# Layer 0 of a four-layer graph kernel: VectorE's work for a row's own sum ranked ahead of its other work, small side products and rank sums issued one row later

## Chip, cores and metric

The kernel runs on one core of a Trainium2 chip. The metric is the device time of one execution in microseconds (us): the median of three runs. Before the change it is 1355.77 us (1353.71 to 1357.23).

## What is computed

`x` is 2708 x 512, `adj` is a sparse, symmetrically placed 2708 x 2708 matrix with a diagonal. Four layers follow each other; each takes `h = relu(layernorm(x))`, does a graph operation with it and adds the result to `x`. The change touches layer 0 alone:

```python
h = jnp.maximum(_layernorm(x), 0.0)
mask = adj > 0
head = mask / sqrt(sum(mask * mask, axis=-1))      # one number per row, on the entries
inc = adj + head
x = x + (inc @ h) / sum(inc, axis=-1)
```

Layer 1 is an attention with the mask of `adj`, which this kernel serves by taking, for each row, the value row of its largest entry. Layer 2 is two products with `adj`, layer 3 one product with `adj != 0` divided by column counts. Layers 1 to 3 also use the lists of nonzero columns that layer 0 makes.

## The kernel before

**Tiles and stages.** The 2708 rows make 22 tiles of 128 rows (the last has 20); I call a tile of rows a row. Layer 0 is one Python loop over `m` in 0 to 21 (L854 to L912), written out in full. Each pass emits the sum of row `m` on TensorE (L865 to L869): first the products with whole tiles of `adj_t` (`inc`), then those with gathered columns (`incl`). All 22 tiles are whole for rows 0 to 2 (`LEAD`); later rows take 6 down to 0 whole tiles (`WHOLE`) and 5 to 8 gathered chunks (`CHUNKS`; row 21 takes 2). For each piece VectorE makes `inc = (a > 0) * rb + a` in `add_head`, with two instructions: L698 and L706. `incidence(m + 1)` (L688), which holds these, is emitted ahead of the sum of row `m`.

**What follows a row's sum.** VectorE adds it to `x` (L879), then `norm` (L191) takes its statistics (L194, L196, L199, L201, with a square root and the final scaling on ScalarE, L198 and L204). The result `hn` is transposed on TensorE one pass later (`after`, L210) and multiplied with the value weights two passes later (L176). `yo` (L810) is then stored to the DRAM table `y`, which layer 1 gathers from.

**Statistics of later rows.** In the same pass `stats_to` (L762) does the statistics of a row that lies up to eight further on: sign and counts on ScalarE (`row_norm`, L583, L587), the row's sum on ScalarE (`row_sum`, L611), the row's largest entry and its place on VectorE (`attended`, L622 to L624). In `row_norm`, for rows 6 to 20, the 128 x 128 block on the diagonal is taken care of at once: VectorE clears the diagonal in the sign block (L592) and picks the diagonal (L595), TensorE multiplies the sign block with a column of ones (L599), and VectorE turns that into `diag_c` (L600).

**Lists of nonzero columns.** After every third row, `count` (L315) adds up the signs of the three rows on TensorE (L325) and ScalarE copies the counts (L341, L343, L345). `rank_blocks` (L391) follows at once: VectorE takes the block sums `rk`, `sums` (L399), TensorE adds the blocks ahead with `ahead_of` (L403), ScalarE copies that (L404), VectorE scans (L405) and sets the end (L406), and SP issues four stores to `rank_b` (L409). Later passes read the ranks back (`load_ranks`, L445) and find the columns (`search`, L448, with the instruction L461); `do_next` (L751) takes one job from the queue `todo` for each row of statistics. `gathers_to(m + 2)` (L790) then has GpSimd gather the entries of row `m + 3` (`gather_adj`, L635) and the rows of `h` of row `m + 2` (`gather_rows`, L654).

**End of layer 0.** From row 14 on, rows 3, 4, 5, 0, 1, 2 (`LATE`), whose slabs were given up, are loaded again and get their signs counted (`count_signs`, L565, held back by a one-element copy of the current `xt`, L182) and their largest entry found. The ranks of row 21 and of rows 1 and 2 are made in `rank_rows` with a long scan (L424); the columns of rows 1 and 2 are searched and gathered for the later layers, and a weight is split in three (L215 to L225). Then `idx` is copied (L914), and layer 1 begins with gathers of `y` by `idx` (L1172).

**What sets the order.** Each engine has one queue in a fixed order. That order is made when the program is built: a planner runs through it with its own estimates of durations, and takes for each engine, of the instructions that are ready by these estimates, the one with the lowest number `tc.cur_priority`. This number grows in the order in which the Python code emits. `tc.issue_after(ins)` adds that what the block emits on the engine of `ins` stands behind it in the queue.

Of the kernel before, what the change touches and what calls it, by code (L numbers as in the profile page):

```python
# [2 lines left out]

# [6 lines left out]
FP = mybir.dt.float32  # L10
# [7 lines left out]
ALU = mybir.AluOpType  # L18
# [17 lines left out]

DENSE = 6
LEAD = 3
HEAD = 3
WHOLE = (6, 6, 6, 6, 6, 6, 4, 4, 4, 4, 4, 4, 3, 3, 3, 4, 4, 4, 3, 3, 3, 0)  # L40
CHUNKS = (0, 10, 9, 8, 7, 7, 7, 7, 7, 6, 6, 6, 6, 6, 6, 5, 5, 5, 5, 5, 5, 2)
# [3 lines left out]
def kernel(  # L45
# [181 lines left out]
    def split_w(pool, raw, tag, first=None):  # L227
# [5 lines left out]
            split_b(*(part[:, c, :] for part in w), raw[:, c, :])  # L233
        return w

    short = ctx.enter_context(ExitStack())
    wset = short.enter_context(tc.tile_pool(name="wset", bufs=1))

# [5 lines left out]
    with tc.tile_pool(name="l0_slab", bufs=2) as slabs, tc.tile_pool(  # L244
# [146 lines left out]
        def rank_blocks(ms, last_block):  # L391

            wide = layout(ms[0] // GROUP)[1]
            row_end = hp.tile([P, WIDE + 1], HF, name="rk")
            rk, end = row_end[:, :wide], row_end[:, wide : wide + 1]
            sums, offs = (wp.tile([P, 1], FP, name=name) for name in ("sums", "offs"))
            nc.vector.tensor_scalar(  # L399
                rk, last_block, 1.0, None, op0=ALU.min, op1=ALU.add, accum_out=sums  # L400
            )
            ahead = ps_list.tile([P, BLK], FP, name="list")
            nc.tensor.matmul(ahead[:, :1], ahead_of, sums, start=True, stop=True)  # L403
# [168 lines left out]
        def row_norm(m):  # L572


            n = rows(m)
            ar = slab[m]

            cnt, sum_sgn = cnts[:, m : m + 1], sums_sgn[:, m : m + 1]
            if m in LATE:
                cnt = sum_sgn = wp.tile([P, 1], FP, name="sum_sgn", bufs=4)  # L580
            rn, deg = (wp.tile([P, 1], FP, name=name, bufs=10) for name in ("rn", "deg"))
            sgn = slabs.tile([P, N], BF, name="sgn", bufs=GROUP)
            nc.scalar.activation(sgn[:n], ar[:n], AF.Sign, accum_out=sum_sgn[:n])  # L583
            if m in LATE:
                nc.vector.tensor_scalar_max(cnt[:n], cnt[:n], 0.0)
            else:
                nc.scalar.activation(sgn[:n], sgn[:n], AF.Relu, accum_out=cnt[:n])  # L587
            nc.scalar.activation(rn[:n], cnt[:n], AF.Sqrt, bias=tiny[:n])
            nc.vector.reciprocal(rn[:n], rn[:n])
            if alone(m):  # L590
                cols = slice(m * P, (m + 1) * P)
                nc.vector.tensor_tensor(sgn[:, cols], sgn[:, cols], off_diag, ALU.mult)  # L592
                picked = wp.tile([P, P], FP, name="dg")
                d = diag[:, m : m + 1]
                nc.vector.scalar_tensor_tensor(  # L595
                    picked, ar[:, cols], 1.0, ident, op0=ALU.mult, op1=ALU.mult, accum_out=d
                )
# [90 lines left out]
        def incidence(m):  # L688

            n = rows(m)  # L690
            rn = row[m][0]
            rb = ps_small.tile([P, P], FP, name="rb")
            nc.tensor.matmul(
                rb[:, :n], rn[:n].to_broadcast([n, P]), ident[:n, :n], start=True, stop=True
            )

            def add_head(inc, a, k, num):
                nc.vector.scalar_tensor_tensor(  # L698
                    inc,
                    a,  # L700
                    0.0,
                    rb[:k, :n].unsqueeze(1).to_broadcast([k, num, n]),
                    op0=ALU.is_gt,
                    op1=ALU.mult,
                )
                nc.vector.tensor_tensor(inc, inc, a, ALU.add)  # L706

            pairs = []
            if m >= LEAD:
                ts = tiles_d[: dense_of(m)]  # L710
                pieces = [ts[i : i + PIECE0] for i in range(0, len(ts), PIECE0)]
            else:
                pieces = in_order if m + 1 < LEAD else dense_last
            for ts in pieces:
                at, k = blocks.pop(m) if m in blocks else load_block(m, ts)
                d = (slice(0, k), slice(0, len(ts)), slice(0, n))
                inc = slabs.tile([P, PIECE0, P], FP, name="inc", bufs=3)
                add_head(inc[d], at[d], k, len(ts))
                pairs += [(inc[:k, i, :n], h0[t][:k]) for i, t in enumerate(ts)]
            if alone(m):  # L720
                c = diag_c[:, m : m + 1]
                by = wp.tile([P, 3], FP, name="by")
                nc.scalar.activation(by[:, 2:3], c, AF.Sign)
                nc.scalar.activation(by[:, 2:3], by[:, 2:3], AF.Identity, scale=rn, bias=c)
                nc.scalar.activation(by[:, :2], kept[:, :, m], AF.Copy, scale=by[:, 2:3])
                own = wp.tile([P, D], FP, name="own", bufs=1)
                nc.scalar.activation(own, xs[m], AF.Relu, scale=by[:, 0:1], bias=by[:, 1:2])
                pairs.append((ident, own))
            if m >= LEAD:
                ac, gs = gathers.pop(m)  # L730
# [15 lines left out]
        listable = set()  # L746


        todo = []
# [12 lines left out]
        def stats_to(m):  # L762


            while normed[0] <= order_n.index(m):
# [88 lines left out]
        for m in range(NT):  # L854
# [10 lines left out]
            for i, (a, g) in enumerate(pairs):  # L865
                product = nc.tensor.matmul(  # L866
                    acc[:n], a, g, start=(i == 0), stop=(i == len(pairs) - 1)
                )
                first_of_sum = first_of_sum if i else product.ins  # L869
            if m + 1 < LEAD:  # L870
                stats_to(m + 1)
                incs[m + 1] = incidence(m + 1)
            if m > 1:
                with tc.issue_after(first_of_sum):
# [4 lines left out]
            nc.vector.scalar_tensor_tensor(  # L879
                xt[:n], acc[:n], row.pop(m)[1][:n], xt[:n], op0=ALU.mult, op1=ALU.add  # L880
            )
# [1071 lines left out]
```

## Time and profile before

| | us |
|---|---|
| median of three runs | 1355.77 |
| the profiled execution, whole | 1431.05 |
| its span, first to last instruction | 1429.2 |
| TensorE busy in the span | 1218.8 (85%) |
| VectorE busy | 924.7 (65%) |
| ScalarE busy | 693.2 (49%) |
| GpSimd busy | 673.6 (47%) |
| mean granted TensorE clock | 0.925 |

The last sum of layer 0 ends at 488 us of the span, and the first product of layer 1 starts at 526.91 us.

How to read it: a group's row gives line, engine, operation, what is written and read, count, busy time, mean duration, then the idle time of that engine just before, and what ended it. "PE" is TensorE, "PEld" its weight loads, DVE VectorE, ACT ScalarE, POOL GpSimd, SP the engine that only issues transfers. A float32 product shows as two MATMUL records. In the list of waits a row reads: who waited, for whom, us in total, times, the longest. In a timeline: start, busy time, engine, line, operation, and in brackets the idle time before and what ended it. In the table by stretches: bounds, length, then busy time of PE, PEld, DVE, ACT, POOL, the granted TensorE clock, the busy share of the transfer engines and GB/s. "remote" as a releaser means that the trace knows a semaphore's update but no work or transfer that made it at that time.

### The profile page before, as it was taken

To read this page: it belongs to the slowest core of one execution; us is meant where nothing else is said; L and a number is where in the kernel's file an instruction comes from. 1 tells how busy PE (TensorE), PEld (TensorE's weight loads), DVE (VectorE), ACT (ScalarE), POOL (GpSimd) and SP (SyncE) were. 2 spreads that over 40 slices of the span, in tenths; PEclk is the share of its full clock that TensorE was granted. 3 is DMA by queue.
4 is the path that set the end of the run, shared out by engine and by line. 5 is a ranking of instruction groups with operands and counts; after the bars stand their busy time and mean duration, and the time that the engine had idled before them with its cause. 6 is when DMAs were issued, how large, how long until landed. Compare 5 with 4: busy or idle time off the path is not lost. (4 is left out here: it accounts for less than half of the span.)

```text
span 1429.2 us, 15148 instructions
## 1 busy us (share of the span) xinstructions
PE 1218.8 (85%) x4223; PEld 726.3 (51%) x4223; DVE 924.7 (65%) x1859; ACT 693.2 (49%) x1098; POOL 673.6 (47%) x703
## 2 busy tenths in 40 slices
PE   4985977769896848999989999899999999958797
PEld 2332433324343326765655655466666666646575
DVE  4664977768899857952343446356667685746576
ACT  5873563648635636642232224245555554634353
POOL 2245457555667441116645543245445344167663
PEclk9977998789988969999999999999999999979898
DMA  9976898778979477638888887856566666488785
GB/s 342 350 251 225 283 302 277 246 249 293 322 253 335 168 254 266 220 128 272 259 261 255 274 248 239 273 177 219 194 212 193 198 190 207 137 313 249 248 250 163
DMA packets 179342, 349.92 MB, mean 245 GB/s; under 512 B 22795, under 2 KB 85525, under 8 KB 175517
## 3 DMA queue, kind: packets, MB, share of 16 engines
q1 hardware_dynamic: 131648, 201.72, 41.5%
q0 software_dynamic: 46032, 145.05, 32.6%
q10 hardware_dynamic: 1568, 2.10, 0.4%
q8 instruction: 35, 0.57, 0.2%
q14 instruction: 59, 0.48, 0.1%
HBM read 285.97 MB, written 62.82 MB: 244 GB/s over the span
## 5 line engine op out<-in xcount | busy, mean ns | idle before, releaser
L1047 POOL DMA_INDIRECT gg<-g2d,idx_g x130 | 141.2, 1086 | 197.1 <-PE aggs L1110 149.3
L1110 PE MATMUL aggs<-gg,ac 128*128 128x512 f32 (+1 forms) x520 | 231.3, 593 | 3.2 <-DMA gg<-g1d,idx_g 2.1
L1047 POOL DMA_INDIRECT gg<-g1d,idx_g x130 | 130.7, 1005 | 159.1 <-PE aggs L1110 86.5
L635 POOL DMA_INDIRECT ac<-in_adj_t_dram,idx_a x130 | 132.7, 1021 | 91.9 <-issue 37.3
L866 PE MATMUL acc<-h,inc 128*128 128x512 f32 (+1 forms) x276 | 143.0, 664 | 37.4 <-DVE inc L706 29.2
L1110 PEld LDWEIGHTS aggs<-gg,ac 128*128 128x128 f32 (+1 forms) x520 | 97.0, 188 | 113.6 <-issue 102.2
L654 POOL DMA_INDIRECT h<-h0d,idx_g x111 | 114.8, 1034 | 83.7 <-PE acc L866 40.8
L866 PE MATMUL acc<-h,incl 128*128 128x512 f32 (+1 forms) x222 | 106.0, 620 | 0.8 <-issue 0.8
L866 PEld LDWEIGHTS acc<-h,inc 128*128 128x128 f32 (+1 forms) x276 | 54.9, 212 | 101.0 <-issue 60.2
L1075 DVE SCALAR_TENSOR_TENSOR ac<-ac,diag_c,bias 128x512 f32<-128x512 f32 x30 | 22.6, 754 | 100.8 <-DMA ac<-g1d 59.1
L1047 POOL DMA_INDIRECT gg<-hidr,idx_g x62 | 70.7, 1140 | 34.6 <-issue 20.8
L176 PE MATMUL yacc<-wvo,hT 128*128 128x512 f32 (+1 forms) x176 | 83.9, 615 | 1.7 <-ACT hT L211 1.0
L1106 PE MATMUL agg<-ghi,a_hi 128*128 128x512 f32 x180 | 77.3, 429 | 0.0
L1106 PE MATMUL agg<-glo,a_lo 128*128 128x512 f32 x180 | 73.4, 408 | 4.2 <-ACT glo L225 4.2
L1106 PE MATMUL aggs<-gs,a_s 128*128 128x512 f32 x180 | 73.1, 406 | 1.3 <-DVE gs L222 1.3
L990 DVE SCALAR_TENSOR_TENSOR v_lo<-pt,v_hi 128x512 fp32r<-128x512 f32 (+1 forms) x88 | 57.0, 658 | 16.2 <-ACT v_hi L989 13.9
L866 PEld LDWEIGHTS acc<-h,incl 128*128 128x128 f32 (+1 forms) x222 | 41.8, 195 | 50.0 <-issue 47.1
L623 DVE MAX8 tops<-ar 128x8 f32<-128x2708 f32 (+1 forms) x22 | 65.4, 2971 | 0.0
L624 DVE FIND_INDEX8 at_top<-tops,ar 128x8 uint32<-128x2708 f32 (+1 forms) x22 | 65.3, 2969 | 0.0
L989 ACT ACTIVATE v_hi<-pt 128x512 fp32r<-128x512 f32 (+1 forms) x88 | 48.2, 575 | 29.0 <-PE pt L983 22.1
L1139 DVE SCALAR_TENSOR_TENSOR u<-aggs,u 128x512 f32<-128x512 f32 x42 | 28.9, 687 | 50.9 <-PE aggs L1110 37.7
L1010 PE MATMUL main<-wb,v_hi 128*128 128x512 f32 (+1 forms) x176 | 56.7, 444 | 5.2 <-ACT v_hi L989 3.4
(355 smaller groups left out, 2777.9 us busy)
## 6 DMA issues: line engine op xcount, KB each, us to landing
ar<-in_adj_dram SPq DMA_DIRECT2D x27, 1354.0 KB
raw<-in_adj_t_dram SPq DMA_DIRECT2D x92, 192.0 KB
slot<-x SPq DMA_DIRECT2D x41, 256.0 KB
at<-in_adj_t_dram SPq DMA_DIRECT2D x26, 256.0 KB
h<-in_x_dram SPq DMA_DIRECT2D x21, 256.0 KB
h0d<-h POOLq DMA_DIRECT2D x21, 256.0 KB
xt<-in_x_dram SPq DMA_DIRECT2D x21, 256.0 KB
x<-xt SPq DMA_DIRECT2D x21, 256.0 KB
```

The lines of the kernel that those rows point to most:

```text
L176: nc.tensor.matmul(acc[:n], hT[:, c, :n], w[:, c, :], start=(c == 0), stop=(c == NCD - 1))
L623: nc.vector.max(tops[:n, m, :], ar[:n])
L624: nc.vector.max_index(at_top[:n, m, :], tops[:n, m, :], ar[:n])
L635: nc.gpsimd.indirect_dma_start(out=ac[:, c, :n], out_offset=None, in_=adj_units, element_offset=dense_of(m) * P * N + m * P, in_offset=bas ...
L654: nc.gpsimd.indirect_dma_start(out=g, out_offset=None, in_=h0d[:, :], in_offset=bass.IndirectOffsetOnAxis(ap=index_g(m)[:, c : c + 1], axi ...
L866: product = nc.tensor.matmul(acc[:n], a, g, start=(i == 0), stop=(i == len(pairs) - 1))
L989: nc.scalar.activation(hi[d], pt[d], AF.Relu, scale=UP)
L990: nc.vector.scalar_tensor_tensor(lo[d], pt[d], 0.0, hi[d].bitcast(FP), op0=ALU.max, op1=ALU.subtract)
L1010: nc.tensor.matmul(acc[:n], a[:, c, :n], b[:, c, :], start=first and c == 0, stop=last and c == NCD - 1,)
L1047: nc.gpsimd.indirect_dma_start(out=gs[c], out_offset=None, in_=gd[:, :], in_offset=bass.IndirectOffsetOnAxis(ap=index_g(m)[:, c : c + 1], ...
L1106: turn(nc.tensor.matmul(acc[:n], a[:k, i, :n], b[:k], start=st, stop=sp))
L1110: nc.tensor.matmul(mixed[:n], a, g, start=(c == 0 and not dense_of(m)), stop=(c == len(chunks) - 1),)
```

## The change

It has three parts. First, a large constant is added to the priority number of everything and taken away again inside `with soon():`, so that what stands there ranks ahead of all else that is ready: `add_head` (L698, L706), and the addition to `x` with `norm` (L879, L194 to L204, the two ScalarE instructions among them). Second, the product L599 with L600 becomes a job in a list `unmixed`, emitted by `diagonals()` at the next row of statistics, behind the first product of the sum then current. Third, `rank_blocks` ends after L399; the rest (L403 to L409) becomes `rank_rest`, a job at the head of its group's searches in `todo`, and stands behind the first product of the sum then current. `do_next` takes a `rank_rest` along when it comes next after the job it was asked for, reads ranks ahead for two searches instead of one, and takes two jobs per pass for one pass more near the end. The first group, rows 3 to 5, does its `rank_rest` at once.

```diff
+SOONER = 1 << 20
...
+    @contextmanager
+    def soon():
+        tc.cur_priority -= SOONER
+        yield
+        tc.cur_priority += SOONER
+
+    tc.cur_priority += SOONER
...
             nc.vector.tensor_scalar(
                 rk, last_block, 1.0, None, op0=ALU.min, op1=ALU.add, accum_out=sums
             )
+            return partial(rank_rest, ms, row_end, sums)
+
+        def rank_rest(ms, row_end, sums):
+
+            wide = layout(ms[0] // GROUP)[1]
+            rk, end = row_end[:, :wide], row_end[:, wide : wide + 1]
+            offs = wp.tile([P, 1], FP, name="offs")
             ahead = ps_list.tile([P, BLK], FP, name="list")
             nc.tensor.matmul(ahead[:, :1], ahead_of, sums, start=True, stop=True)
...
-                others = ps_list.tile([P, BLK], FP, name="list")
-                nc.tensor.matmul(others[:, :1], sgn[:, cols], ones_b, start=True, stop=True)
-                nc.vector.scalar_tensor_tensor(
-                    diag_c[:, m : m + 1], others[:, :1], 0.0, d, op0=ALU.is_equal, op1=ALU.mult
-                )
+                unmixed.append(partial(diagonal, m, sgn))
...
+        def diagonals():
+
+            for job in unmixed:
+                if first_of_sum[0] is None:
+                    job()
+                else:
+                    with tc.issue_after(first_of_sum[0]):
+                        job()
+            unmixed.clear()
...
             def add_head(inc, a, k, num):
-                nc.vector.scalar_tensor_tensor(
...
-                nc.vector.tensor_tensor(inc, inc, a, ALU.add)
+                with soon():
+                    nc.vector.scalar_tensor_tensor(
...
+                    nc.vector.tensor_tensor(inc, inc, a, ALU.add)
...
         def do_next(num=1):
+            if num and todo[num:] and todo[num].func is rank_rest:
+                num += 1
             for job in todo[:num]:
                 if job.func is search and job.args[0] not in ranks_of:
                     load_ranks(job.args[0])
-                job()
+                if job.func is rank_rest:
+                    with tc.issue_after(first_of_sum[0]):
+                        job()
+                else:
+                    job()
...
-            if todo and todo[0].func is search and todo[0].args[0] not in ranks_of:
-                load_ranks(todo[0].args[0])
+            for job in todo[:2]:
+                if job.func is not search:
+                    break
+                if job.args[0] not in ranks_of:
+                    load_ranks(job.args[0])
...
+                diagonals()
                 row_norm(t)
...
-                            rank_blocks(list(masks), last_block)
+                            rest = rank_blocks(list(masks), last_block)
+                            if t == FIRST[-1]:
+                                rest()
+                            else:
+                                todo.append(rest)
...
-            nc.vector.scalar_tensor_tensor(
-                xt[:n], acc[:n], row.pop(m)[1][:n], xt[:n], op0=ALU.mult, op1=ALU.add
-            )
-            hns[m] = wp.tile([P, D], FP, name="hn")
-            norm(wp, xt, n, hns[m])
+            with soon():
+                nc.vector.scalar_tensor_tensor(
+                    xt[:n], acc[:n], row.pop(m)[1][:n], xt[:n], op0=ALU.mult, op1=ALU.add
+                )
+                hns[m] = wp.tile([P, D], FP, name="hn")
+                norm(wp, xt, n, hns[m])
             store(m, xt)
             if normed[0] == NT:
-                do_next(2 if NT - 8 < m < NT - 5 else 1)
+                do_next(2 if NT - 8 < m < NT - 4 else 1)
             stats_to(min(2 * m + 6, m + 8, NT - 1))
+            if normed[0] == NT and m > NT - 9:
+                diagonals()
```

More of the change, by code (lines that the diff above doesn't have):

```diff
@@ L1 @@
-from contextlib import ExitStack
+from contextlib import ExitStack, contextmanager
 from functools import partial
@@ L397, in rank_blocks @@
             rk, end = row_end[:, :wide], row_end[:, wide : wide + 1]
-            sums, offs = (wp.tile([P, 1], FP, name=name) for name in ("sums", "offs"))
+            sums = wp.tile([P, 1], FP, name="sums")
             nc.vector.tensor_scalar(
@@ L597, in row_norm, with diagonal @@
                 )
-                others = ps_list.tile([P, BLK], FP, name="list")
-                nc.tensor.matmul(others[:, :1], sgn[:, cols], ones_b, start=True, stop=True)
-                nc.vector.scalar_tensor_tensor(
-                    diag_c[:, m : m + 1], others[:, :1], 0.0, d, op0=ALU.is_equal, op1=ALU.mult
-                )
-            masks[m], row[m] = sgn, (rn, deg, cnt)
+                unmixed.append(partial(diagonal, m, sgn))
+            masks[m], row[m] = sgn, (rn, deg, cnt)
+        unmixed = []
+        def diagonal(m, sgn):
+            others = ps_list.tile([P, BLK], FP, name="list")
+            nc.tensor.matmul(
+                others[:, :1], sgn[:, m * P : (m + 1) * P], ones_b, start=True, stop=True
+            )
+            nc.vector.scalar_tensor_tensor(
+                diag_c[:, m : m + 1],
+                others[:, :1],
+                0.0,
+                diag[:, m : m + 1],
+                op0=ALU.is_equal,
+                op1=ALU.mult,
+            )
+        def diagonals():
[6 more added lines that the diff above has]
+            unmixed.clear()
         def row_sum(m):
@@ L697, in add_head @@
             def add_head(inc, a, k, num):
[L698 to L704, printed above, removed]
-                )
-                nc.vector.tensor_tensor(inc, inc, a, ALU.add)
+                with soon():
+                    nc.vector.scalar_tensor_tensor(
+                        inc,
+                        a,
+                        0.0,
+                        rb[:k, :n].unsqueeze(1).to_broadcast([k, num, n]),
+                        op0=ALU.is_gt,
+                        op1=ALU.mult,
+                    )
+                    nc.vector.tensor_tensor(inc, inc, a, ALU.add)
             pairs = []
@@ L746 @@
         listable = set()
-        todo = []
+        todo, first_of_sum = [], [None]
         def do_next(num=1):
+            if num and todo[num:] and todo[num].func is rank_rest:
+                num += 1
             for job in todo[:num]:
@@ L868 @@
                 )
-                first_of_sum = first_of_sum if i else product.ins
+                first_of_sum[0] = first_of_sum[0] if i else product.ins
             if m + 1 < LEAD:
@@ L873 @@
             if m > 1:
-                with tc.issue_after(first_of_sum):
+                with tc.issue_after(first_of_sum[0]):
                     after(m - 2, None)
@@ L878 @@
             xt = xs.pop(m)
-            nc.vector.scalar_tensor_tensor(
-                xt[:n], acc[:n], row.pop(m)[1][:n], xt[:n], op0=ALU.mult, op1=ALU.add
-            )
-            hns[m] = wp.tile([P, D], FP, name="hn")
-            norm(wp, xt, n, hns[m])
+            with soon():
+                nc.vector.scalar_tensor_tensor(
+                    xt[:n], acc[:n], row.pop(m)[1][:n], xt[:n], op0=ALU.mult, op1=ALU.add
+                )
+                hns[m] = wp.tile([P, D], FP, name="hn")
+                norm(wp, xt, n, hns[m])
             store(m, xt)
             if normed[0] == NT:
-                do_next(2 if NT - 8 < m < NT - 5 else 1)
+                do_next(2 if NT - 8 < m < NT - 4 else 1)
             stats_to(min(2 * m + 6, m + 8, NT - 1))
+            if normed[0] == NT and m > NT - 9:
+                diagonals()
             gathers_to(m + 2)
```

## The prediction

> **What bounds the kernel now.** I read in this order: the page's engine shares, a table of layer 0 by stretches, TensorE's list of waits, then the timelines around the longest waits. The change touches only layer 0, the first 501 us of 1429; the rest is taken as unchanged.
>
> ```profile
> PE 1218.8 (85%) x4223; PEld 726.3 (51%) x4223; DVE 924.7 (65%) x1859; ACT 693.2 (49%) x1098; POOL 673.6 (47%) x703
> ```
>
> ```profile
> 246.00:254.00 8.00, 0.00 (x0) 0.00 (x0) 0.00 (x0) 0.00 (x0) 5.88 (x7) 0.60 0.33 80
> 260.00:308.00 48.00, 45.93 (x143) 21.24 (x143) 44.20 (x85) 33.05 (x46) 28.74 (x30) 0.95 0.94 315
> 320.00:385.00 65.00, 64.13 (x191) 29.13 (x191) 59.16 (x112) 47.66 (x67) 40.45 (x41) 0.95 0.92 316
> 400.00:430.00 30.00, 30.00 (x79) 13.79 (x78) 29.35 (x44) 12.34 (x20) 20.05 (x16) 0.98 0.76 262
> 448.00:480.00 32.00, 31.76 (x78) 14.43 (x79) 32.00 (x54) 16.20 (x19) 16.43 (x17) 0.93 0.80 309
> ```
>
> In stretches without a stall TensorE is full (64.13 of 65 us), and VectorE nearly so (59.16 of 65; 32.00 of 32 from 448 on). So the change can win what TensorE stands still, and VectorE has little room to give. Where TensorE stands still:
>
> ```profile
> PE acc L866 <- DVE inc L706: 29.2, 3, 15.7
> PE list L403 <- DVE rk L399: 29.1, 4, 15.2
> ...
> PE pt L210 <- ACT hn L204: 7.1, 2, 5.9
> ```
>
> All three are the change's targets. The timelines (TensorE, then VectorE, ScalarE, GpSimd) say how far each wait is one of order:
>
> ```profile
> 260.11 0.59 PE L403 MATMUL list<-sums,ahead_of 128*128 128x1 f32 x2 [15.18 <-DVE rk L399]
> ...
> 447.87 2.08 PE L866 MATMUL acc<-h,inc 128*128 128x512 f32 x2 [11.28 <-DVE inc L706]
> ...
> 498.98 1.12 PE L210 MATMUL pt<-ident,hn 128*128 128x128 f32 x4 [5.92 <-ACT hn L204]
> ```
>
> ```profile
> 259.29 0.76 DVE L399 TENSOR_SCALAR_CACHE_REDUCE rk<-counts 128x581 f16<-128x581 bf16 x1 [18.07 <-ACT counts L343]
> ...
> 430.33 0.53 DVE L698 SCALAR_TENSOR_TENSOR inc<-at,rb 128x384 f32<-128x384 f32 x1
> ...
> 447.27 0.54 DVE L706 TENSOR_TENSOR inc<-inc,at 128x384 f32<-128x384 f32 x1
> ...
> 487.11 2.97 DVE L624 FIND_INDEX8 at_top<-tops,ar 128x8 uint32<-128x2708 f32 x1
> 490.00 1.38 DVE L879 SCALAR_TENSOR_TENSOR xt<-acc,deg,xt 128x512 f32<-128x512 f32 x2
> ```
>
> ```profile
> 258.55 0.59 ACT L341 CAST counts<-list 128x512 bf16<-128x512 f32 x1 [19.27 <-remote]
> ```
>
> ```profile
> 472.40 0.94 POOL L635 DMA_INDIRECT ac<-in_adj_t_dram,idx_a  x1 [11.00 <-DVE inc L706]
> ...
> 507.91 0.57 POOL L645 DMA_DIRECT2D lst<-ac  x1 [1.21 <-DMA ac<-in_adj_t_dram,idx_a]
> 514.58 1.34 POOL L1172 DMA_INDIRECT slot<-y,idx  x1 [6.11 <-ACT wb L225]
> ```
>
> Two things are to be seen. At 430 the two halves of one `inc` lie 17 us apart, with scan, MAX8, FIND_INDEX8 and weight splits between them: pure order. But at 260 TensorE waits for VectorE, VectorE for ScalarE, and ScalarE for "remote", although the counts that it copies (L325) ended at 242.0; from 246 to 254 no engine but GpSimd works. That stall has no work behind it. The profiled execution is 1431.05 us, 75.3 over the median of 1355.77, so stalls of about this kind must be missing in the runs that count.
>
> [...] L403 held up the products of the sum behind it for 15.18 us, L399 VectorE for 18.07. [...] 0.60 granted in 246 to 254, and the pair at 447.87 took 2.08 us, where an undisturbed one takes 1.02. [...]
>
> **The change part by part**, in us of the profiled execution.
>
> (a) `rank_rest` one row later. TensorE's four waits are 0.8, 1.7, 15.2 and 11.5. Work explains only the way from the counts to L403: L341 0.59, L343 0.22, L399 0.76 and its 0.08, together 1.65, partly beside remaining products; the undisturbed wait was 1.67. The first (0.8) belongs to rows 3 to 5, whose rest isn't moved. I count 3 x 1.7 = 5.1; bounds 1.7 and 28.3. Nothing is added: per group two products (0.29 each), L404 0.15, L405 1.2 to 1.4, L406 0.15, four stores on SP (1.2 to 1.9 of its time) and the reads of ranks move by one pass (13 to 15 us), past the next row's loads on SP. By the code a search then runs in pass k-4 instead of k-5, and GpSimd's `gather_adj(k)` is emitted in pass k-3: one pass of cover is left. While it holds, cost 0; bounds -2 and +2 per group for SP's new order (5 groups).
>
> (b) The diagonal products. TensorE waited 1.4, 1.0, 0.8 and 0.7 ahead of L599: 3.9, all gone if the sign block is a row old. The 15 pairs (0.17 each on TensorE and VectorE) remain. L600 no longer holds up VectorE behind a fresh product (it stood 5.9 once, "remote", not counted). Count 3.9; bounds 2 and 8.
>
> (c) `add_head` ahead. Of 29.2, 15.7 ended with a VectorE that itself stood 12.9 for "remote": not counted. The short wait of 2.2 and one of 2.6 put down to "issue" just before an `inc` product are of this kind: I count 3 of 4.8. The 11.3 at 447 with the half clock after it (2.08 + 3.01 for 6 records, against 1.02 + 1.88) is 13.5 for TensorE. But VectorE is full there until 480; what is pulled ahead pushes the rest back. So it counts in (d).
>
> (d) Rows 15 to 21 and the passage to layer 1. The `xt` of row 20 stood from about 484.5 to 490.0 behind MAX8 and FIND_INDEX8. Its followers are a ScalarE sign pass, the last MAX8 and FIND_INDEX8 (to 501.05), `idx`, and the store of `y` at 511.4. With `xt` and `norm` in front, row 21's `y` can be stored some 12 earlier. Late next is GpSimd, which gathers rows 1 and 2 until 508.5, so the gathers of `y` (514.58) win 6 at most, if VectorE's searches for rows 1 and 2 don't slip. VectorE's idle time from 430 to 501 (about 5.4: 71 less 65.6 busy) is the other ceiling. Count 5; bounds -7 and 13.
>
> (e) `norm` ahead in the middle: the other wait on `hn` (7.1 less 5.9), 1.2. Bounds 0 and 5.
>
> (f) The price of a fixed order. L879 is placed where the planner thinks the sum is done; if it is later, everything behind it on VectorE (MAX8, searches, next statistics) stands. The page shows no such wait now (0.0 ahead of L879), so no row prices it: 0 at best; at worst all VectorE's free 1.3 per row (5.84 in 65 us, 4.5 rows) for 16 rows, 20. I take 3, because the inserted work is short (0.7 to 1.1 each).
>
> Sum: 5.1 + 3.9 + 3 + 5 + 1.2 - 3 = 15.2. That is 1431.05 to 1416 for a profiled execution. I counted only waits that work explains, so I carry it over whole: 1355.8 - 15.2 = 1340.6.
>
> **Rivals.** *All that the profile shows is recovered*: 28.3 + 3.9 + 29.2 + 7.1 = 68.5, less what belongs to the 75.3 that the runs don't have. If a bit over half is real, 42 are won: 1314. For it: each long stall stands at an instruction that is moved. Against it: "remote". *Given back*: VectorE is 91 to 100% busy, so TensorE's waits only change their place; also what would be seen if the planner's estimates leave the pairs apart. 1353 to 1358. *Slower: searches too late.* Own-sum work is about 5.2 per row (L879 0.73, norm 1.2, four `add_head` halves 0.6 to 0.95). With the ranks a pass later too, a search ends after GpSimd comes to gather; then GpSimd, and a row later TensorE, wait. It decides once a search slips by more than the pass left, 13 us; VectorE's full stretch after 400 is the place. Price 5.2 for each of five groups, 26, against some 13 still won: +13, 1369. Against it: own-sum work delays a search once and doesn't add up while VectorE has any room.
>
> **How the numbers follow.** About 0.3% (4 us) is what a measurement of this kernel can tell from no change. The forecast, 1327 to 1351: 0.56; all recovered, 1305 to 1327: 0.13; given back, within 4 us: 0.13; slower, 1360 to 1375: 0.18. Its single time is 1340.5. Faster 0.69, same 0.13, slower 0.18. The range 1316 to 1363 leaves out about half of each outer case, 0.16. Its ends agree with the bounds: all low ends add to about 30 lost, all high ones to over 60 won, and neither is likely together. The likeliest case's own range is 1327 to 1351.
>
> **What would show it.** (a) right: L403 without a wait on `rk`, L325 followed by products. (b): no wait ahead of L599. (c): L706 within 2 us of its L698 everywhere, no wait of `acc` on `inc` over 3. (d): L879 of rows 20 and 21 at once after their sums, the first gather of `y` some 15 us earlier in the span, L635 for rows 1 and 2 its new limit. (f): idle time ahead of L879. Wrong: GpSimd waiting for `idx_a` in rows 9 to 20, or TensorE for gathered `h` or `incl`; long "remote" stalls going from the profile while the median stays.

## The result, and the profile after

The changed kernel takes 1372.95 us (1369.01 to 1378.26, 4 runs), the kernel before 1356.28 us beside it: a ratio of 1.0139, interval 1.0107 to 1.0170. It is **slower by 1.4%**, outside the predicted range (1316 to 1363). The profiled execution after took 1374.74 us, its span is 1373.0. The kernel before ran at two levels in these measurements, 1353.5 to 1356.3 us in most sets of runs and 1428.4 and 1432.2 us in the sets of e8 to e11 and of e12 to e15, so each ratio is taken inside one set.

The profile of before that the prediction was read from ran 75 us over the median. The kernel before was therefore profiled again: span 1353.1 us, no idle time put down to "remote". I compare with this second profile; "before" means it from here on. Line numbers are those of each run's own kernel: L698, L706 and L879 of before are L737, L745 and L933 after, and differ by a few lines in the runs below. An engine "stands" when it is idle and waits. The engines' busy time, on the page of after:

```profile
PE 1207.2 (88%) x4223; PEld 719.0 (52%) x4223; DVE 925.1 (67%) x1859; ACT 694.1 (51%) x1098; POOL 671.5 (49%) x703
```

VectorE has the same work as ever (924.7 in the first profile of before). Where the time went is told by one stretch, from 90 us to VectorE's last FIND_INDEX8 of the statistics, which ends at 447.0 before and at 470.1 after. First before, then after, in the table by stretches:

```profile
90.00:447.00 357.00, 312.56 (x936) 141.82 (x935) 328.31 (x600) 223.17 (x308) 246.73 (x237) 0.96 0.88 306
```

```profile
90.00:470.00 380.00, 320.58 (x935) 145.68 (x934) 328.70 (x601) 222.71 (x310) 245.31 (x241) 0.91 0.85 288
```

VectorE is busy 328.3 and 328.7 us, the stretch is 23 us longer: VectorE stands 51.3 us instead of 28.7. TensorE stands 59.4 instead of 44.4, and its mean granted clock goes from 0.96 to 0.91; nearly the same number of products keeps it busy for 320.6 us instead of 312.6. Behind that stretch nothing more is lost: GpSimd's first gather of `y` for layer 1 starts 20.8 us later, and the span is 19.9 longer.

```profile
460.73 1.29 POOL L1172 DMA_INDIRECT slot<-y,idx  x1 [4.44 <-ACT wb L225]
```

```profile
481.53 1.08 POOL L1228 DMA_INDIRECT slot<-y,idx  x1 [4.93 <-DVE wb L223]
```

TensorE's waits from 90 us to the end of layer 0, before and after (waiting, for whom, us in all, times, longest):

```profile
PE acc L866 <- DVE inc L706: 21.5, 5, 12.2
PE list L599 <- DVE sgn L592: 6.2, 4, 2.2
PE pt L210 <- ACT hn L204: 5.9, 1, 5.9
PE list L403 <- DVE rk L399: 4.0, 4, 2.3
...
PE yacc L176 <- ACT hT L211: 1.4, 2, 0.7
```

```profile
PE pt L211 <- ACT hn L205: 17.9, 4, 6.5
PE yacc L177 <- ACT hT L212: 11.0, 2, 10.5
PE rb L731 <- DVE incl L737: 10.2, 2, 6.0
PE list L418 <- DVE rk L407: 6.3, 1, 6.3
PE acc L919 <- DVE inc L745: 3.8, 2, 3.7
PE list L333 <- DVE sgn L607: 3.8, 3, 1.9
PE list L621 <- DVE sgn L607: 3.6, 3, 1.8
```

The change shortens the waits that it aims at: that for `inc` falls from 21.5 to 3.8, that of the diagonal product (L599, now L621) for the sign block from 6.2 to 3.6. But part of the latter only moved: the product that counts the signs (L333) now waits 3.8 for the same block. And other waits have come: for `hn`, for `hT`, for the buffer of `rb` that an `incl` still reads. VectorE's own waits say why. In the same stretch, before and after:

```profile
DVE inc L698 <- DMA at<-in_adj_t_dram: 7.3, 4, 4.4
DVE rstd L199 <- ACT rstd L198: 5.4, 4, 2.8
DVE ends L455 <- DMA ranks<-rank_b: 4.8, 5, 2.4
```

```profile
DVE ends L470 <- DMA ranks<-rank_b: 14.6, 6, 4.4
DVE rstd L200 <- ACT rstd L199: 9.5, 3, 7.9
DVE incl L737 <- DMA ac<-in_adj_t_dram,idx_a: 9.3, 3, 5.3
DVE inc L737 <- DMA at<-in_adj_t_dram: 6.3, 4, 4.6
DVE xt L933 <- PE acc L919: 4.4, 4, 1.9
```

Added up, VectorE stands 15.0 us at own-sum instructions (`inc`, `incl`, `xt`, `norm`) before and 31.8 after (the 9.5, 9.3, 6.3 and 4.4 above and 2.3 more at `inc`), and 5.0 and 14.6 at searches that wait for ranks. (The experiments below show that the loss goes with the first of these and not with the second.) One place, ahead of the sum of row 12, in the timelines of ScalarE, VectorE and TensorE:

```profile
295.11 2.46 ACT L598 ACTIVATE sgn<-ar 128x2708 bf16<-128x2708 f32 x1 [10.76 <-DMA ar<-in_adj_dram]
297.48 0.19 ACT L598 ACTIVATION_READ_ACCUMULATOR sgn<-ar 128x1 f32 x1
297.57 0.28 ACT L199 ACTIVATE rstd<-mv,eps 128x1 f32<-128x1 f32 x1
```

```profile
288.98 0.17 DVE L197 BATCH_NORM_AGGREGATE mv<-stats 128x2 f32<-128x6 f32 x1
...
297.88 0.16 DVE L200 RECIPROCAL rstd<-rstd 128x1 f32<-128x1 f32 x1 [7.90 <-ACT rstd L199]
297.96 0.54 DVE L745 TENSOR_TENSOR inc<-inc,at 128x384 f32<-128x384 f32 x1
```

```profile
301.05 1.11 PE L211 MATMUL pt<-ident,hn 128*128 128x128 f32 x4 [5.49 <-ACT hn L205]
```

ScalarE's square root (0.28 us) stood in its queue behind a sign pass whose slab came late: its input `mv` was there at 289.15, ScalarE was idle until the sign pass began at 295.11 (10.76 us), and the square root began at 297.57. The reciprocal stood ranked in front on VectorE, and 7.9 us of VectorE's time went by with `inc`, a search and the next statistics behind it; the first half of that `inc` had ended at 289.06. Here neither engine ran what stood behind the instruction that waited, and this is what the ranking in front runs into.

### The profile page after: what moved, and what is told of

It reads as the page before. It is cut to its first block, busy times and chain, and to the rows that moved or that the text cites. A ratio compares the mean times of both kernels' runs of the same rounds, so it can differ in the third digit from the quotient of the medians.

```text
span 1373.0 us, 15139 instructions
## 1 busy us (share of the span) xinstructions
PE 1207.2 (88%) x4223; PEld 719.0 (52%) x4223; DVE 925.1 (67%) x1859; ACT 694.1 (51%) x1098; POOL 671.5 (49%) x703
## 4 chain that ended last, share of the span: by engine, by line
PE 39%; DMA 12%; issue 6%; DVE 5%; ACT 2%; POOL 1%; SPq 0%; DVEq 0%; ACTq 0%; POOLq 0%
PE aggs L1166 12%; PE main L1066 7%; PE agg L1162 5%; PE mixed L1066 3%; PE aggs L1162 2%; PE aggs L1376 2%; PE agg L1376 2%; DMA gg<-hidr,idx_g 2%; DMA ac<-g1d 2%; PE pt L1039 2%; DMA g2d<-go 2%; DMA ac<-g2d 2%; DMA raw<-in_adj_t_dram 1%; POOL gg L1103 1%; PE pt L1376 1%
## 5 line engine op out<-in xcount | busy, mean ns | idle before, releaser
L1103 POOL DMA_INDIRECT gg<-g2d,idx_g x130 | 146.4, 1126 | 190.1 <-PE aggs L1166 137.3
L673 POOL DMA_INDIRECT ac<-in_adj_t_dram,idx_a x130 | 127.2, 978 | 71.9 <-issue 34.1
L692 POOL DMA_INDIRECT h<-h0d,idx_g x111 | 119.4, 1076 | 71.5 <-PE acc L919 38.9
L919 PE MATMUL acc<-h,inc 128*128 128x512 f32 (+1 forms) x276 | 135.5, 634 | 9.2 <-DVE inc L745 3.8
L919 PE MATMUL acc<-h,incl 128*128 128x512 f32 (+1 forms) x222 | 102.8, 612 | 0.0
L1131 DVE SCALAR_TENSOR_TENSOR ac<-ac,diag_c,bias 128x512 f32<-128x512 f32 x30 | 22.6, 752 | 103.1 <-DMA ac<-g1d 55.5
L1103 POOL DMA_INDIRECT gg<-hidr,idx_g x62 | 65.5, 1056 | 29.4 <-issue 13.4
L598 ACT ACTIVATE sgn<-ar 128x2708 bf16<-128x2708 f32 (+1 forms) x22 | 54.0, 2453 | 25.0 <-DMA ar<-in_adj_dram 24.5
```

Source lines behind the costliest of these rows:

```text
L673: nc.gpsimd.indirect_dma_start(out=ac[:, c, :n], out_offset=None, in_=adj_units, element_offset=dense_of(m) * P * N + m * P, in_offset=bas ...
L692: nc.gpsimd.indirect_dma_start(out=g, out_offset=None, in_=h0d[:, :], in_offset=bass.IndirectOffsetOnAxis(ap=index_g(m)[:, c : c + 1], axi ...
L919: product = nc.tensor.matmul(acc[:n], a, g, start=(i == 0), stop=(i == len(pairs) - 1))
L1103: nc.gpsimd.indirect_dma_start(out=gs[c], out_offset=None, in_=gd[:, :], in_offset=bass.IndirectOffsetOnAxis(ap=index_g(m)[:, c : c + 1], ...
```

## Experiments

Ratios are to the kernel before, measured in the same set of runs; "us" below is the ratio's distance from 1 times the time of before. The idle time of VectorE runs from 90 us to its last FIND_INDEX8 of the statistics, and the last column is the part of it that ends at own-sum instructions (`inc`, `incl`, `xt`, `norm`). Both are left out for e8 to e15, whose traces have idle stretches put down to "remote", like the first profile of before. They come from one profiled execution each, which can lie some us from the median: that of e5 took 1362.3 us with a median of 1369.8, that of e17 1350.0 with 1357.7.

| run | ratio, 95% interval | us | VectorE idle | of it at own-sum work |
|---|---|---|---|---|
| the change | 1.0139 (1.0107 to 1.0170) | +18.9 | 51.3 | 31.8 |
| e0 before | 0.9983 (0.9953 to 1.0013) | -2.3 | 28.7 | 15.0 |
| e1 first part | 1.0206 (1.0164 to 1.0248) | +27.9 | 54.1 | 39.8 |
| e2 second part | 1.0022 (1.0003 to 1.0042) | +3.0 | 31.5 | 9.6 |
| e3 third part | 1.0018 (0.9990 to 1.0046) | +2.4 | 38.2 | 14.0 |
| e4 heads in front | 1.0070 (1.0044 to 1.0097) | +9.5 | 34.4 | 18.1 |
| e5 xt, norm in front | 1.0115 (1.0087 to 1.0142) | +15.6 | 40.9 | 17.9 |
| e6 all but incl | 1.0090 (1.0057 to 1.0123) | +12.2 | 48.3 | 22.3 |
| e7 second and third | 1.0037 (1.0019 to 1.0055) | +5.0 | 32.4 | 10.1 |
| e8 second halves | 0.9993 (0.9966 to 1.0021) | -1.0 | | |
| e9 last two rows | 0.9993 (0.9963 to 1.0023) | -1.0 | | |
| e10 first part by 64 | 1.0187 (1.0148 to 1.0227) | +26.7 | | |
| e11 control | 1.0013 (0.9985 to 1.0041) | +1.9 | | |
| e12 more VectorE | 1.0140 (1.0096 to 1.0184) | +20.1 | | |
| e13 more TensorE | 1.0042 (1.0021 to 1.0062) | +6.0 | | |
| e14 behind by 64 | 1.0105 (1.0061 to 1.0149) | +15.0 | | |
| e15 e8 and e9 | 0.9968 (0.9942 to 0.9994) | -4.6 | | |
| e16 the same again | 1.0035 (1.0011 to 1.0059) | +4.8 | 34.4 | 10.2 |
| e17 change, cut down | 1.0028 (1.0009 to 1.0048) | +3.8 | 32.7 | 12.9 |

The last column divides the runs: where VectorE stands 17.9 us or more at own-sum work, the loss is 9.5 or more; where it stands 15.0 or less, the loss is 5.0 or less. Its standing at searches doesn't: it is 14.6 us after the change, but 14.3 in e17 and 13.8 in e3, which lost 3.8 and 2.4.

**e0: the kernel before, again.**

> The kernel before, unchanged, for a second profile of it. If the long stalls that end in 'remote' belong to the one profiled execution of 1431 us, this profile's span is within 5 us of 1354, no idle stretch of TensorE in layer 0 ends in 'remote', and the first gather of y starts near 460 (514.6 less about 54 of such stalls). If they belong to the kernel, they are here again. Time: 1356 by both.

Span 1353.1, nothing "remote", first gather of `y` at 460.73. So the long stalls of the first profile are not the kernel's own, and leaving them out of the sum was right; the change could not win them.

**e1 to e3: each part alone.** In e1 the other two parts are undone:

```diff
-                unmixed.append(partial(diagonal, m, sgn))
+                diagonal(m, sgn)
...
-                            if t == FIRST[-1]:
-                                rest()
-                            else:
-                                todo.append(rest)
+                            rest()
```

(`do_next` is then as before, too.) e2 and e3 undo one of these and have `SOONER = 0`.

> Only the first part of the change: own-sum work ranked in front; diagonal products and ranks' block sums as before. Theory 'own-sum work placed too early' (the work in front takes VectorE and ScalarE from the statistics, the searches and the incidences of the next row): +8 to +17 us, most of the loss, with TensorE waiting for hn, hT and incl as it does in the kernel after. Theory 'searches too late' (the ranks' sums a row later are what costs): 0 to -10 us here.

> Only the second part: the sign block's product moved into the next row's sum. My prediction's term: -4 us, bounds -8 and -2. A theory that any move of this small kind shifts the planner's order elsewhere: anything from -5 to +5, with waits at places that the edit doesn't touch.

> Only the third part: the ranks' block sums a row later, searches and loads of ranks as in the kernel after. Theory 'searches too late': +10 to +20 us, with GpSimd waiting for idx_a and TensorE for gathered h. Theory 'own-sum work placed too early': within 5 us of the kernel before, or faster by the 5 that my prediction gave this term.

The first part costs 27.9 us alone, more than I expected and more than the whole change. The others measured 2 to 3, the third with an interval that holds no change. "Searches too late" falls as the main cause: in e3 the searches end up to 20 us later than before, for 2.4 us. The second part's -4 did not come either. With the other two the first part loses less (18.9). In e1 TensorE waits 29.3 us at the diagonal product for VectorE, after the change 3.6; that fits, but no run isolates it.

What goes wrong in e1 is seen in VectorE's waits (90 to 475 us) and in the timelines of VectorE and GpSimd:

```profile
DVE incl L737 <- DMA ac<-in_adj_t_dram,idx_a: 18.2, 4, 7.6
DVE inc L737 <- DMA at<-in_adj_t_dram: 6.7, 2, 4.8
DVE xt L930 <- PE acc L916: 6.5, 4, 2.6
```

```profile
250.85 0.17 DVE L197 BATCH_NORM_AGGREGATE mv<-stats 128x2 f32<-128x6 f32 x1
258.62 0.95 DVE L737 SCALAR_TENSOR_TENSOR incl<-ac,rb 128x768 f32<-128x768 f32 x1 [7.60 <-DMA ac<-in_adj_t_dram,idx_a]
...
263.36 2.98 DVE L661 MAX8 tops<-ar 128x8 f32<-128x2708 f32 x1
...
266.45 2.98 DVE L662 FIND_INDEX8 at_top<-tops,ar 128x8 uint32<-128x2708 f32 x1
```

```profile
252.39 0.94 POOL L673 DMA_INDIRECT ac<-in_adj_t_dram,idx_a  x1 [0.30 <-issue]
253.64 0.94 POOL L673 DMA_INDIRECT ac<-in_adj_t_dram,idx_a  x1 [0.30 <-issue]
```

GpSimd issues a gather every 1.25 us here, 0.94 busy and 0.30 between. These are the last two of the six that this `incl` reads; when VectorE came to it, at 251.0, three had been issued, and the wait ends 5 us after the issue of the sixth. VectorE has come 7.6 us too early and began nothing of what stands behind it in that time; the MAX8 began at 263.36. What that does to the two streams of work, from the traces (end of the row's sum on TensorE; end of the nth FIND_INDEX8 of the statistics):

| us | before | e1 | after |
|---|---|---|---|
| sum of row 4 | 176.6 | 171.0 | 170.3 |
| sum of row 7 | 224.9 | 218.2 | 229.2 |
| sum of row 12 | 301.3 | 321.9 | 315.1 |
| sum of row 21 | 434.0 | 454.6 | 447.6 |
| 3rd statistics | 134.2 | 131.6 | 129.5 |
| 8th | 216.3 | 232.3 | 224.1 |
| 13th | 296.5 | 332.2 | 316.6 |
| 22nd | 447.0 | 475.3 | 470.1 |

The sums run ahead at first, by 6 us at row 4. The statistics fall behind; then the sums stop being ahead.

**e4 and e5: the halves of the first part**, with the other two parts undone as in e1.

```diff
             def add_head(inc, a, k, num):
-                with soon():
...
```

is e5 (xt and norm stay in front); e4 takes away the other `with soon():`.

> Of the first part only one half: add_head (both halves of every inc and incl) ranked in front, xt and norm not; nothing else changed. Theory 'VectorE stands at work put in front whose input isn't there': in the run with the whole first part VectorE stood 18.2 us at incl for gathered ac, so most of its +27 us is here: +12 to +25 us, with VectorE's standing ahead of incl over 10 us. Rival 'the row's end does it' (xt and the five hops of norm between VectorE and ScalarE): -5 to +5 us here.

> The other half: xt and norm ranked in front, add_head not. Theory 'VectorE stands at work put in front whose input isn't there': xt stood 6.5 us in all for its sum and rstd 1.6 for ScalarE in the run with the whole first part, so 0 to +10 us. Rival 'the row's end does it': +15 to +27 us.

+9.5 and +15.6: both halves cost, and together about what e1 does. I had put the larger share on the heads; that was wrong. With the heads alone VectorE hardly stands at `incl` (2.2 us). In e5 it stands at `xt`, and at searches (as long as in e2, which lost 3.0):

```profile
DVE ends L470 <- DMA ranks<-rank_b: 11.3, 5, 4.2
DVE xt L930 <- PE acc L916: 7.1, 3, 4.2
```

**e6: all in front but incl.**

```diff
-                add_head(inc, ac, P, CHUNKS[m])
+                add_head(inc, ac, P, CHUNKS[m], ahead=nullcontext)
```

> The whole first part, but incl, the incidence made from gathered columns, left at its old rank; inc (from a block loaded two rows ahead), xt and norm in front. Theory that the gathers are what the planner has wrong: VectorE's 18.2 + 3.8 us ahead of incl go, so +3 to +10 us instead of +27. Theory that own-sum work in front delays the statistics whatever it is: still +15 to +27, with the last FIND_INDEX8 of the statistics 20 or more us later than before, as it is with the whole first part (28).

+12.2 instead of +27.9. The waits for gathered columns (18.2 in e1) are gone, and so are 15.7 us. VectorE's idle time as a whole fell by only 5.8 us, that at own-sum work by 17.5. This is the clearest single cause. The rest, 12.2, is between my two expectations: the last FIND_INDEX8 is still 18 us late, with VectorE standing 9.3 us at `xt` and 9.5 at `inc`.

**e7: second and third part.** `SOONER = 0` in the kernel after.

> Second and third part together, the first left out. If the parts add up (each measured at +3 us), +4 to +8 us, and then the 8 us by which the whole change is better than its first part alone come from how the parts act on each other. If the order of the work shifts by chance with any edit, anything between -8 and +10.

+5.0: they add up to what each measured alone.

**e8 and e9: pieces of the first part that can hardly make VectorE stand.** e8 has `with soon():` around the second instruction of `add_head` alone; e9 has

```diff
+            with soon() if m >= NT - 2 else nullcontext():
```

> Only the second instruction of add_head (inc + block) ranked in front, in all rows; everything else as in the kernel before. Its inputs are the first instruction's output on the same engine and a block that this one has read already, so VectorE can never stand at it. Theory 'VectorE is the bound, and its standing sets the time': TensorE's wait for inc in row 18 (12.2 us in the second profile of before) shrinks, but VectorE has the same work to do by the end, so -4 to +3 us, and VectorE's idle time from 90 us to its last FIND_INDEX8 stays within 4 us of before's 28.7. Theory of my prediction (TensorE's stall at row 18 and its half clock are what is won): -6 to -13 us.

> xt and norm ranked in front for rows 20 and 21 alone; everything else as in the kernel before. By my prediction's step for the passage to layer 1: y of row 21 is stored some 5 to 8 us earlier, and the first gather of y, which came 4.44 us after GpSimd was free in the second profile of before, wins at most those 4.4: -2 to -4.4 us. Theory that the steps behind hn (transposes, hT, yo, at their old rank) then queue behind the last sign passes on ScalarE, as hT did in the kernel after (10.5 us): 0 to +6 us.

Neither moved by more than its interval. e8 excludes the -6 to -13 of my prediction's reading, but it didn't test what it was for: TensorE still waits 10.9 us in row 18, since here the first half of `inc` comes late. At the second halves, 61 instructions in layer 0, VectorE stood 0.1 us, at the first halves of `inc` 14.5. Its VectorE idle time can't be held against 28.7 either, because of the "remote" stretches. e9's interval, -5.3 to +3.3 us, can't tell -2 to -4.4 from nothing.

**e10 and e11: how far in front, and a control.** e10 is e1 with `SOONER = 64`; e11 puts only the 1x1 minimum of each row in front.

> The whole first part, but with a rank only 64 places further ahead instead of 1,048,576, so that own-sum work passes the last emitted instructions and not a whole pass; nothing else changed. If the loss comes from how far the work is put in front: between 0 and +15 us, with VectorE idle between 28.7 and 54.1. If any reordering costs about the same: +20 to +30.

> A control: of all VectorE's work only the 1x1 minimum behind each incl (0.13 us, once per row) is ranked in front. It does nothing for any theory of mine. If the order of the kernel before is good by selection and any edit loses some of it, as the second and third part (+3 each) might: +2 to +6 us. If not: within 2 us.

64 places cost +26.7, as much as a million: beyond 64 places the distance doesn't matter (shorter ones weren't tried). The control stays within noise, so not every edit of the order costs.

**e12 and e13: the same load on one engine or the other.**

```diff
+            nc.vector.max(tops[:n, m, :], ar[:n, :1200])
             nc.vector.max(tops[:n, m, :], ar[:n])
```

```diff
+            a, g = pairs[0]
+            nc.tensor.matmul(acc[:n], a, g, start=True, stop=True)
+            nc.tensor.matmul(acc[:n, : D // 2], a, g[:, : D // 2], start=True, stop=True)
             for i, (a, g) in enumerate(pairs):
```

> The kernel before with a redundant MAX8 over 1200 columns ahead of each MAX8 (22 of about 1.3 us on VectorE, 29 us in all; its result is overwritten). Theory 'VectorE is the bound of layer 0': +18 to +32 us. Theory of my prediction (TensorE full, its waits are what counts, VectorE nearly full): +5 to +15.

> The kernel before with the first product of each row's sum made one and a half times more (22 of about 1.29 us on TensorE, 28 us in all; its result is overwritten by the product proper). Theory 'VectorE is the bound of layer 0': TensorE has 44 us of idle time from 90 us on, so +0 to +14 us. Theory of my prediction: +18 to +30.

VectorE got 30.8 us more (the group below), and the run took 20.1 more (13.7 to 26.4): about 0.65 us per us. TensorE's products for the sums took 279.9 us, against 256.8 to 261.8 in three traces with the sums unchanged and such stretches (the first profile of before, e9, e11): some 20 more, and the run 6.0 more (3.0 to 8.9), about 0.3 per us. So VectorE's time is likely the dearer; the factor is rough, as the two intervals divided by the added work overlap. Both were measured among idle stretches "remote", and it isn't shown that the prices are the same without them.

```profile
L623 DVE MAX8 tops<-ar 128x8 f32<-128x1200 f32 (+1 forms) x22 | 30.8, 1399 | 0.0
```

**e14: own-sum work behind.** e10 with `SOONER = -64`.

> The first part turned round: own-sum work ranked 64 places behind its place in the kernel before, which puts statistics and searches in front of it; nothing else changed. Theory 'own-sum work in front holds up the statistics and makes VectorE stand': -6 to +6 us, VectorE's idle time up to the last FIND_INDEX8 at 28.7 or less. Theory 'any larger reordering costs, before is well ordered': +10 to +25.

+15.0, against my -6 to +6. So it isn't the direction alone. Where the 15.0 arises, the trace doesn't tell. TensorE's longest waits, for the ranks' sums, have ScalarE's "remote" waits at the counts behind them (TensorE, then ScalarE):

```profile
PE list L418 <- DVE rk L407: 27.3, 3, 13.9
```

```profile
ACT counts L349 <- remote: 30.5, 3, 18.7
```

e9, which lost nothing, has the same pair with 27.0 and 27.4 us.

**e15 and e16: e8 and e9 together, twice; e17: the change with its first part cut down to them.**

> The two pieces of the first part at which VectorE can hardly stand, together: the second instruction of add_head in front in all rows, xt and norm in front for rows 20 and 21. If each is worth what e8 and e9 measured: within 2 us of the kernel before. If my prediction's passage to layer 1 was right in itself and only hidden by the idle stretches in e9: -3 to -6 us, and the first gather of y by 456 in the profile.

> The same kernel as in the run with second half and last rows together, once more beside the kernel before. If the 0.3% is a gain of the order itself: -2 to -7 us again, the first gather of y earlier than before's. If it was chance: within 3 us.

> The kernel after, with its first part cut down to those two pieces; the diagonal products and the ranks' sums moved as in the change. If the loss of 17 us is the first part's reach (work in front at which VectorE stands): second and third part measured +5 together and the two pieces -4.6, so -4 to +5 us. If the second and third part lose on their own when combined with any first part: +8 to +17.

The same kernel gave -0.3% in one set and +0.35% in the other, with intervals that don't meet: it is no gain that I can show, and effects of half a per cent are not settled by one set here. That holds for e2, e3, e7, e13 and e17 too. e17 takes 15 of the change's 18.9 us back: its VectorE stands 32.7 us, against 51.3, and 12.9 at own-sum work, against 31.8. No version tried beats the kernel before in a way that a second set confirmed.

## Why the prediction was wrong

**The sum by parts.** For the first part I had forecast a gain of 6.2 us, (c), (d) and (e) less (f); alone it lost 27.9. For the other two, (a) and (b), I had a gain of 9.0; together they measured +5.0. So the larger error lies in the first part.

**The reading of the limit.** I saw that both engines were nearly full and then added up TensorE's waits, as if each were worth its length. The waits did shrink where I said; the time did not follow. The 23 us of the longer stretch can be booked on either engine: VectorE, with its work fixed at 327 to 331 us in all traces without "remote" stretches, stands 22.6 longer; TensorE stands 15.0 longer and is busy 8.0 longer at its lower clock. e12 against e13 says that VectorE is likely the dearer one, and over all runs the loss goes with VectorE's standing at own-sum work. Its idle time as a whole is a poorer guide, as e6 against e1 shows.

**Term (f), the price of a fixed order, failed.** "I take 3, because the inserted work is short": no row of before had idle time ahead of L879. But the page shows waits at places where the planner had put things late; it can't show what comes of putting them early. Measured: 16.8 us more standing at own-sum instructions after the change (31.8 against 15.0), which my bound of 20 held, and 24.8 more with the first part alone (39.8), which it didn't. Leaving `incl` at its old rank (e6) took 17.5 us of that standing and 15.7 of the loss away. I also priced `xt` alone (4.4 us of standing after the change); at `incl`, waiting for gathers, VectorE stood 9.3, and at `rstd`, waiting for ScalarE, 9.5.

**(a)** Before, L403's waits for `rk` in layer 0 are 4.3 us in all (5), not the 29.1 of the first profile; after, 7.4 (2), of which one is 6.3. Nothing is won. Cost of the later ranks: I had 0, with 2 per group at worst; VectorE stands 13.8 us for ranks and their like in e3 and 5.0 before, and the third part gives +2.4, not -5.1.

**(b)** TensorE's waits at the diagonal product, for whatever VectorE or ScalarE work, fell from 8.6 to 3.6 us, but L333 now waits 3.8 for the sign block, and the second part alone is +3.0, not -3.9. In e2 the waits for `inc` are larger instead (26.5 us). Given back, as the rival said.

**(c), (d), row 18.** Behind the wait there the clock was about half: in the first profile of before 0.55 was granted from 447.8 to 453.0 and 1.00 from 453 to 460, and in the second the first pair behind the 12.2 us took 2.08 us, the one at 399.47 1.02. In e1 and after the change TensorE no longer waits there; as I had it, the rest of VectorE's work is then later. The passage to layer 1 got longer by 7.2 us (from row 21's last product to the first gather of `y`: 26.7 before, 33.9 after), against -5. Two steps failed. First, `xt` of row 20 didn't follow its sum at once: it began 10.2 us after the last product, behind three searches and a MAX8 (5.5 us before the change). Being ranked in front helps only among what the planner counts as ready, and it had not counted `xt` so. After, TensorE and VectorE:

```profile
435.46 2.31 PE L919 MATMUL acc<-h,incl 128*128 128x512 f32 x5
```

```profile
447.95 0.73 DVE L933 SCALAR_TENSOR_TENSOR xt<-acc,deg,xt 128x512 f32<-128x512 f32 x1
```

Second, I forgot that the step after `xt` and `norm`, `hT`, kept its old rank on ScalarE, behind four sign passes. After, ScalarE and TensorE:

```profile
463.36 2.45 ACT L585 ACTIVATE sgn<-sgn 128x2708 bf16<-128x2708 bf16 x1
...
465.81 0.57 ACT L212 ACTIVATE hT<-pt 128x512 f32<-128x512 f32 x1
```

```profile
466.44 6.44 PE L177 MATMUL yacc<-wvo,hT 128*128 128x512 f32 x8 [10.54 <-ACT hT L212]
```

**(e)** The wait for `hn` grew from 5.9 us in one piece to 17.9 in four. At rows 14 and 19 (6.5 and 2.5) the planner had put the transposes one sum earlier on TensorE than before, and `hn` was not there yet. At rows 10 and 20 (5.5 and 3.3) they stand where they stood before, and `hn` itself came late; row 10 is the place with the reciprocal above.

**Right:** the "remote" stalls as no part of the gain; the wait for `inc`; the amount of the slower rival (1369), but by luck: its mechanism is not what happened. The sign that I had named for it, GpSimd waiting for `idx_a` in rows 9 to 20, is not in the trace of after, and late searches alone (e3) cost little.

**What stays open.** Of the first part's 27.9 us, 15.7 are tied to `incl` by e6. The rest lies in `xt`, `norm` and `inc` in front, but e14 shows that a shift the other way costs 15.0, so how much is due to standing and how much to leaving this particular order is not told apart. That the runs with more standing at own-sum work are those that lost more speaks for standing, but each of them also has that work in front. Taking the waits away at their source, by earlier gathers for one, wasn't tried.

## What to carry to other kernels

Where two engines are both nearly full, ask by adding work which one a microsecond is dearer on, before adding up waits of the other. Work ranked in front in a fixed order must have its inputs there by the clock and not by the planner's estimate: leave in place what waits for a gather or another engine (VectorE stood 7.6 us at one `incl` in e1, 7.9 at one reciprocal after the change). To put in front what reads only what its own engine has just made did no harm that e8 could measure (-1.0 us, interval -4.9 to +3.0), but brought no gain either. A chain that is hurried must be hurried to its end, on each engine that it crosses; that is read from one place of one trace, and no run tested it. And hold an idle time against the time of the same profiled execution: it can lie several us from the median.

## What the runs showed of the hardware that I had not expected

Some traces show waits with no work behind them, put down to "remote", on several engines. In e8 (waits of VectorE, then of ScalarE, layer 0):

```profile
DVE diag_c L624 <- remote: 16.0, 2, 8.5
```

```profile
ACT hT L212 <- remote: 15.3, 3, 7.9
```

What makes them I don't know; the second profile of before has none. They spread: behind 19.27 us of ScalarE at the counts, in the first profile of before at 258.55, come 18.07 us of VectorE waiting for ScalarE and 15.18 of TensorE waiting for VectorE, so that a list of one engine's waits looks like a fault of order (e14).

In the trace of e1 eleven indirect gathers of GpSimd in a row, from 247.40 to 259.88, start 1.25 us apart, the first ten 0.94 busy, with 0.30 between. The six that one `incl` reads there take 7.2 us to issue.
